# Two places for the weights of single expert blocks, an earlier second layer near the end, and a bias gated on ScalarE in a fused attention and mixture-of-experts kernel

## The chip, the cores and the metric

The kernel runs on one core of one Trainium2 chip. The metric is the device time of one execution in microseconds (us). All arithmetic is in fp32. The engines are named as the profile names them: PE (TensorE matmuls), PEld (TensorE weight loads), DVE (VectorE), ACT (ScalarE), POOL (GpSimd) and SP (SyncE, which here issues most of the DMAs).

## The reference

The input x holds 32 batches of 112 tokens with D = 256. The first layer is a gated cross-attention: its latents are the layer norm of x, its keys and values come from 375 context rows and the 112 latents (487 in all), with 16 heads of 64. The second layer is a feed-forward layer with 8 experts, of which each token takes two. What matters for the change is this second layer:

```
xf = layernorm(x).reshape(3584, 256)
scores = softmax(xf @ gate_w); top 2 of 8, divided by their sum
h = gelu(einsum('td,edf->etf', xf, w1) + b1)      # exact gelu, F = 1024
y = einsum('etf,efd->etd', h, w2) + b2
out = sum over the token's two experts of score * y
x = x + tanh(g_ffn) * out
```

## The kernel before

After the attention stage each token's row is scattered to a DRAM array `xg`, once for each of its two experts, so that the rows of an expert lie together. A row carries its 256 values, its gate (column `D`) and the number of its token (column `D + 1`). The expert stage then works through units of rows in an order fixed ahead. Which expert a unit belongs to is read from a table at run time (`number`, the register loads of `L1028`).

There are 21 **pairs** (`PAIRS = 21`, units 0 to 20) of 2 x 128 rows. They use a scheme of seven products of blocks where plain multiplication takes eight (`hidden_pair` and `second_pair`, whose matmuls are `L1255` and `L1317`), with sums of weights made earlier (`ws1`, `ws2`). After them come 18 **single blocks** of 128 rows (`SURE = 18`, units 21 to 38), computed plainly. `hidden(t)` makes the 1024 hidden values in 8 columns of 128, two matmuls each (`L1367`), and each column has a gelu with its bias on ACT (`L1374`). `second(t)` sums 8 matmuls into one bank (`L1382`). The trace has two rows for each of these fp32 matmuls: 32 for `hidden`, 16 for `second`. `combine(t)` adds the bias b2 on DVE (`L1232`), multiplies by the row's gate on DVE (`L1234`), and lets POOL issue a scatter-add of the 128 rows to the output (`add_rows`, `L1207`). The scatter-adds follow one another: each waits until the one before it has landed, since two blocks can hold the same token. Up to three more blocks stand behind a `tc.If`; they are not executed with these inputs.

**Weights.** A single block's weights are four halves of 512 KB: the first layer's two (hidden columns 0 to 511 and 512 to 1023) in the tiles `w_s23` and `w_12_22`, the second layer's two in `t14` (called `b1x`) and `b2x`. Each tile has one buffer, and `w_s23`, `w_12_22`, `t14` and `b2x` are the tiles of the pairs too. The trace shortens their names: `w_s` is `w_s23`, `w` is `w_12_22`, `w_t` is `t14`. SP issues the loads: `fetch_first` (`L1119`) for the first layer, `fetch_second` (`L1135`) for the second. From the second single block on each is conditional: it is done only where the block's expert differs from that of the block before. The loads of a half wait until the matmuls that read the same place are over. `found["w1"]` and `w2_first` are two further places of 1 MB each that held the weights of unit 0 and lie idle afterwards.

**Order.** The instructions of each engine run in the order in which the program writes them (`manual_schedule`). For a single block t the loop `run` writes `hidden(t)`, then the fetch of the first layer of t+1, the transposes of its rows (`turn_rows`, `L1158`, copied by DVE at `L1162`), `second(t - 1)` and `combine(t - 1)`, then the fetch of the second layer of t, and the rows of t+3. ACT issues the loads of the biases (`L1074` for b1, `L1077` for b2) and of the rows (`L1057`), in its queue between the gelus. After the last block `second` and `combine` of block 38 follow directly on those of 37:

```python
        def run(begin, end):
            for t in range(begin, end):
                hidden(t)
                if t + 1 < end:
                    fetch_first(t + 1)
...
                    second(t - 1)
                    combine(t - 1)
                fetch_second(t)
                rows_ahead(t, end)
            second(end - 1)
            combine(end - 1)
```

PSUM's eight banks are used in turn, one for each column of `hidden`. The tiles of the blocks (`hid`, `xsT`, `y`) have two buffers each.

## Time and profile before

| | us |
|---|---|
| median of 3 runs | 1871.33 |
| lowest and highest run | 1870.01, 1871.95 |
| the profiled execution | 1865.82 |
| its span in the profile | 1864.0 |

The mean granted clock of PE was 0.999 of full speed. In the profile a line of a group of instructions gives source line, engine, operation, output <- inputs with the names of the program, and the count; then busy time and the mean of one in ns. A line of the timeline gives its start, its duration, its engine, its line and operation, the number of instructions run together, and in brackets how long the engine had been idle before it and what ended that. `SPq` and `ACTq` are the queues of SP and ACT, where DMAs are issued. The duration of such a row is that of the issue and not of the transfer.

### The profile page before, as it was taken

Reading aid. Unit: us, or ns where it says so; the run is one execution under the profiler, and the core shown is the slowest. Engines: PE = TensorE matmul, PEld = TensorE weight load, DVE = VectorE, ACT = ScalarE, POOL = GpSimd, SP = SyncE. Lnnn points to the kernel's source line nnn. Section 1 sums busy time; section 2 is a strip of 40 time slices with the busy share of each in tenths; the row PEclk is TensorE's granted clock in tenths of the full one; section 3 lists DMA queues with packets and bytes.
Section 4 is the critical chain, followed back from the end, with each engine's and each line's share of the span. In section 5 each row is a group of like instructions: output and inputs, shape, how many; then the busy total and the mean of one; then the engine's idle time right before and its main releaser. Section 6 shows DMA issues by size and latency. Waiting matters only on the chain. (4 is left out here: it accounts for less than half of the span.)

```text
span 1864.0 us, 37204 instructions
## 1 busy us (share of the span) xinstructions
PE 1843.0 (99%) x12336; PEld 1410.6 (76%) x12336; DVE 1377.0 (74%) x2898; ACT 1131.8 (61%) x2718; POOL 969.0 (52%) x1361
## 2 busy tenths in 40 slices
PE   8999999999999999999999999999999999999998
PEld 4667777676677677767677767777677999999887
DVE  6888887888887878788878787888776477754111
ACT  4776666666676767676767676766656344434333
POOL 6433342525354846484556655662334688877212
PEclk9999999999999999999999999999999999999999
DMA  6577767666878888989898988897548876997872
GB/s 207 203 248 250 246 215 235 222 225 205 257 272 252 305 271 275 284 283 306 275 282 276 283 289 285 261 311 241 211 171 295 269 218 179 283 347 213 247 187 42
DMA packets 389747, 462.51 MB, mean 248 GB/s; under 512 B 142984, under 2 KB 279472, under 8 KB 373168
## 3 DMA queue, kind: packets, MB, share of 16 engines
q1 hardware_dynamic: 359568, 432.19, 70.0%
q0 software_dynamic: 11328, 15.33, 4.2%
q10 hardware_dynamic: 18656, 12.58, 2.5%
q8 instruction: 99, 1.62, 0.4%
q14 instruction: 96, 0.79, 0.1%
HBM read 316.05 MB, written 186.96 MB: 270 GB/s over the span
## 5 line engine op out<-in xcount | busy, mean ns | idle before, releaser
L592 ACT ACTIVATE ex<-bank,nmx 128x512 f32<-128x512 f32 x512 | 344.0, 698 | 86.2 <-DVE nmx L583 86.2
L606 ACT ACTIVATE ex<-ex,rc 128x512 f32<-128x512 f32 x512 | 345.1, 730 | 59.4 <-DVE rc L603 58.8
L583 DVE TENSOR_REDUCE nmx<-bank 128x1 f32<-128x487 f32 x512 | 298.3, 655 | 69.8 <-PE bank L573 69.3
L611 DVE STREAM_TRANSPOSE ex<-ex 128x1024 f32<-128x1024 f32 x256 | 314.1, 1227 | 20.3 <-ACT ex L606 20.2
L524 POOL TENSOR_TENSOR vv<-tmpv,vv 128x512 f32<-128x512 f32 x64 | 82.0, 1281 | 403.9 <-ACT vv L512 393.1
L573 PE MATMUL bank<-kT,qTs 64*128 64x487 f32 x1024 | 234.2, 583 | 0.8 <-ACT outT L652 0.3
L635 PEld LDWEIGHTS bank<-exT,vv 128*64 128x64 f32 (+1 forms) x4096 | 197.5, 136 | 29.5 <-issue 24.8
L652 ACT COPY outT<-bank 128x256 f32<-128x256 f32 (+3 forms) x160 | 40.0, 314 | 289.1 <-PE bank L635 289.1
L635 PE MATMUL bank<-exT,vv 128*64 128x112 f32 (+1 forms) x4096 | 211.3, 260 | 0.0
L471 PE MATMUL bank<-tT,wkv_s 128*128 128x487 f32 x378 | 186.5, 576 | 0.5 <-ACT ex L592 0.5
L476 PE MATMUL bank<-wkv_s,tT 128*128 128x256 f32 x768 | 186.5, 379 | 0.0
L476 PEld LDWEIGHTS bank<-wkv_s,tT 128*128 128x128 f32 x768 | 145.8, 190 | 44.0 <-issue 22.5
L1452 POOL TENSOR_TENSOR piece<-piece 128x128 f32<-128x128 f32 x256 | 117.2, 458 | 109.6 <-DMA piece<-in_L_ffn_w_dram 98.3
L573 PEld LDWEIGHTS bank<-kT,qTs 64*128 64x128 f32 x1024 | 98.4, 186 | 95.8 <-issue 70.7
L1207 POOL DMA_INDIRECT out_dram<-y,xs x60 | 93.6, 1559 | 148.7 <-DVE y L1234 64.8
L476 PEld LDWEIGHTS bank<-wkv,kvT 128*128 128x128 f32 x512 | 95.8, 190 | 56.3 <-issue 33.4
L476 PE MATMUL bank<-wkv,kvT 128*128 128x256 f32 x512 | 131.7, 380 | 0.8 <-ACT ex L592 0.6
L471 PE MATMUL bank<-kvT,wkv 128*128 128x487 f32 x252 | 130.1, 598 | 0.0
L521 DVE TENSOR_TENSOR vv<-bank,vv 128x512 f32<-128x512 f32 x192 | 123.4, 668 | 6.9 <-POOL vv L524 6.9
L521 DVE TENSOR_TENSOR kT<-bank,kT 128x487 f32<-128x487 f32 x189 | 116.8, 640 | 15.5 <-PE bank L471 15.2
L1262 ACT ACTIVATE h<-h,b 128x256 f32<-128x256 f32 x160 | 66.1, 495 | 89.5 <-DVE h L1275 89.5
L410 PEld LDWEIGHTS bank<-kvT,wq_sb 128*128 128x128 f32 x512 | 96.8, 190 | 28.1 <-issue 17.0
(299 smaller groups left out, 3654.9 us busy)
## 6 DMA issues: line engine op xcount, KB each, us to landing
turned<-ex SPq DMA_DIRECT2D x128, 1024.0 KB
exT<-turned SPq DMA_DIRECT2D x128, 1024.0 KB
w_t<-ws SPq DMA_DIRECT2D x40, 512.0 KB
w<-in_L_ffn_w_dram SPq DMA_DIRECT2D x38, 512.0 KB
w_b2x<-in_L_ffn_w_dram SPq DMA_DIRECT2D x38, 512.0 KB
ws<-piece SPq DMA_DIRECT2D x64, 256.0 KB
turned_in<-inputs SPq DMA_DIRECT2D x28, 512.0 KB
kvT<-turned_in SPq DMA_DIRECT2D x224, 64.0 KB
```

What stands on the lines that cost most here:

```text
L410: nc.tensor.matmul(ps, lhsT=wq_sb[:, k, i * P : (i + 1) * P], rhs=kvT[g][:, k, :, :S], start=(k == 0), stop=(k == KD - 1),)
L471: nc.tensor.matmul(ps, lhsT=w[:, 0, i * P : (i + 1) * P], rhs=x[:, :NK], start=True, stop=True)
L476: nc.tensor.matmul(ps[:, c, :], lhsT=x[:, (2 * h + c) * P : (2 * h + c + 1) * P], rhs=w[:, 1, i * P : (i + 2) * P], start=True, stop=True,)
L521: nc.vector.tensor_tensor(v[o], ps, v[r], ALU.add)
L573: nc.tensor.matmul(ps[:, :NK], lhsT=qT[b // 2, i][r, b % 2].rearrange("p a i -> p (a i)"), rhs=kT[b, i][r, :], start=True, stop=True,)
L583: nc.vector.tensor_reduce(nmx[b, i][:, j : j + 1], pss[b, i][j][:, :NK], AX.X, ALU.max, negate=True)
L592: nc.scalar.activation(exs[n % EXB][:, :, p, :, j, :], ps[j].rearrange("p (c r k) -> p k c r", c=NCK, r=QW), AF.Exp, bias=nmx[b, i][:, j : ...
L606: nc.scalar.mul(t, t, rc[:, j : j + 1])
L611: nc.vector.transpose(t, t)
L635: nc.tensor.matmul(ps[y * DH : (y + 1) * DH, r, x * S : (x + 1) * S].rearrange("p (a i) -> p a i", a=QB), lhsT=vv[j // 2, c // 2][:m, c % ...
L1207: add = nc.gpsimd.indirect_dma_start(out=outf, out_offset=bass.IndirectOffsetOnAxis(ap=xs[t][:, b, D + 1 : D + 2].bitcast(I32), axis=0), i ...
L1452: nc.gpsimd.tensor_tensor(o, l, r, op) for o, l, r, op in ops
```

## The change

The change has four parts, in the single blocks.

- The first half of each layer's weights gets two places, used by turns. With i = t - 21, the first layer's is a half of `found["w1"]` for even i and `w_s23` for odd i; the second layer's is a half of `w2_first` for even i and `t14` for odd i. The second halves stay in `w_12_22` and `b2x` (for i = 0 in the other halves of `found["w1"]` and `w2_first`). The second half is loaded if the expert differs from the block before. The first half is loaded if the expert of this block or of the block before is new, since its place was filled two blocks ago. Blocks 21 and 22 are loaded in any case.
- The order of the loads moves. All four halves of block 21 are issued at pair 18. The two first-layer halves of block 22 are issued at pair 20. In `run`, after `hidden(t)` come the second half of the first layer of t+1 and the first half of the first layer of t+2; after `second(t - 1)` come the second half of the second layer of t and the first half of the second layer of t+1. New functions `single`, `fetch_single` and `biases_of_single` do this; `single` loads three registers on SP where there were two.
- In the last turn of `run`, `second(37)` and `combine(37)` stand ahead of `hidden(38)`.
- Ahead of `second(t)`, ACT writes b2 times the gate into the unused half of the tile `y` (`gated_bias`); DVE then makes y from the bank, the gate and that half in one instruction instead of two.

```diff
@@ -1064,7 +1064,7 @@
             m, i = unit_of(t)
             e = number(m, i, 0, E - 1, (ET.SP, ET.Activation) if t > 1 else (ET.SP,))
 
-            new = {} if t in (0, 1, EARLY, PAIRS) else {"cond": number(m, i, 2, 1)}
+            new = {} if t in (0, 1, EARLY) else {"cond": number(m, i, 2, 1)}
             return e, new
 
         def fetch_biases(t, e, pool, n, layers=(0, 1)):
@@ -1101,20 +1101,14 @@
 
             e, new = found["e", t] = found.pop(("next", t), None) or expert_of(t)
             fetch_biases(t, e, found["weights"], 2, (0,))
-            if t < PAIRS:
-                s1_, s4_ = (
-                    (n, ws1[bass.ds(e, 1), place].rearrange("o p f -> p (o f)"))
-                    for n, place in (("s1", 3), ("s4", 2))
-                )
-                s23 = "s23", ws1[bass.ds(e, 1), 0:2].rearrange("o s p f -> p (o s) f")
-                order_ = (
-                    ("11", half_of_w1(e, 0, 0)), s23, s1_, ("12_22", rows_of_w1(e, 1)), s4_
-                )
-            else:
-                if t == PAIRS:
-                    wt["11"], wt["12"] = (wt["s23"][:, n] for n in range(2))
-                    wt["21"], wt["22"] = (wt["12_22"][:, n] for n in range(2))
-                order_ = ("s23", columns_of_w1(e, 0)), ("12_22", columns_of_w1(e, 1))
+            s1_, s4_ = (
+                (n, ws1[bass.ds(e, 1), place].rearrange("o p f -> p (o f)"))
+                for n, place in (("s1", 3), ("s4", 2))
+            )
+            s23 = "s23", ws1[bass.ds(e, 1), 0:2].rearrange("o s p f -> p (o s) f")
+            order_ = (
+                ("11", half_of_w1(e, 0, 0)), s23, s1_, ("12_22", rows_of_w1(e, 1)), s4_
+            )
             for n, src in order_:
                 nc.sync.dma_start(wt[n], src, **new)
 
@@ -1122,15 +1116,8 @@
 
             e, new = found.pop(("e", t))
             b2x = "b2x", half_of_w2(e, 1, 0, D)
-            if t < PAIRS:
-                planes = ws2[bass.ds(e, 1)].rearrange("o (a b) p c d -> b p (o a) (c d)", b=2)
-                order_ = ("b11", half_of_w2(e, 0, 0, P)), b2x, ("t14", planes[0]), ("t32", planes[1])
-            else:
-                if t == PAIRS:
-                    wt["b1x"] = wt["t14"].rearrange("p a f -> p (a f)").rearrange(
-                        "p (c d) -> p c d", d=D
-                    )
-                order_ = ("b1x", half_of_w2(e, 0, 0, D)), b2x
+            planes = ws2[bass.ds(e, 1)].rearrange("o (a b) p c d -> b p (o a) (c d)", b=2)
+            order_ = ("b11", half_of_w2(e, 0, 0, P)), b2x, ("t14", planes[0]), ("t32", planes[1])
             for n, src in order_:
                 nc.sync.dma_start(wt[n], src, **new)
             fetch_biases(t, e, found["weights"], 2, (1,))
@@ -1141,6 +1128,30 @@
 
             e, _ = expert_of(0)
             nc.sync.dma_start(w2_first, w2[bass.ds(e, 1)].rearrange("o (c p) d -> p (o c) d", p=P))
+
+        def single(t, cond=True):
+
+            i = t - PAIRS
+            e = number("c", i, 0, E - 1, (ET.SP, ET.Activation))
+            one = two = {}
+            if cond and i > 1:
+                one = number("c", i, 2, 1)
+                one, two = {"cond": one}, {"cond": one | number("c", i - 1, 2, 1)}
+            H = NF // 2
+            room = found["w1"].rearrange("p k (h f) -> p h k f", h=2)
+            b1x = wt["t14"].rearrange("p a f -> p (a f)").rearrange("p (c d) -> p c d", d=D)
+            wt["w1", t] = [(room[:, 0], wt["s23"])[i % 2], wt["12_22"] if i else room[:, 1]]
+            wt["w2", t] = [(w2_first[:, :H], b1x)[i % 2], wt["b2x"] if i else w2_first[:, H:]]
+            found["one", t] = e, two, one
+
+        def fetch_single(t, layer, h):
+            e, *new = found["one", t]
+            dst = wt[("w1", "w2")[layer], t][h]
+            src = columns_of_w1(e, h) if layer == 0 else half_of_w2(e, h, 0, D)
+            nc.sync.dma_start(dst, src, **new[h])
+
+        def biases_of_single(t, layer):
+            fetch_biases(t, found["one", t][0], found["weights"], 2, (layer,))
 
         def weights_ahead():
 
@@ -1227,11 +1238,20 @@
             n = 2 if t == 0 else 1
             sums = found.pop("sums", [])
             do(sums[:1])
-            y = found["tiles"].tile([P, 2, D], F32, tag="y", name=f"y_{t}")
+            y = ys.pop(t, None)
+            if y is None:
+                y = found["tiles"].tile([P, 2, D], F32, tag="y", name=f"y_{t}")
             for b in range(n):
-                nc.vector.tensor_tensor(y[:, b], psy.pop((t, b)), bias[t][1], ALU.add)
-                give((t, b))
-                nc.vector.tensor_scalar(y[:, b], y[:, b], xs[t][:, b, D : D + 1], None, ALU.mult)
+                gate = xs[t][:, b, D : D + 1]
+                if t < PAIRS:
+                    nc.vector.tensor_tensor(y[:, b], psy.pop((t, b)), bias[t][1], ALU.add)
+                    give((t, b))
+                    nc.vector.tensor_scalar(y[:, b], y[:, b], gate, None, ALU.mult)
+                else:
+                    nc.vector.scalar_tensor_tensor(
+                        y[:, b], psy.pop((t, b)), gate, y[:, 1], ALU.mult, ALU.add
+                    )
+                    give((t, b))
                 added = add_rows(t, b, y[:, b])
                 if n == 2:
                     do(sums[b + 1 : b + 2])
@@ -1363,10 +1383,10 @@
             for f in range(NF):
                 ps = psum(P)
                 h, c = divmod(f, NF // 2)
-                for k, w in enumerate((("11", "12"), ("21", "22"))[h]):
+                for k in range(KD):
                     nc.tensor.matmul(
                         ps,
-                        lhsT=wt[w][:, c * P : (c + 1) * P],
+                        lhsT=wt["w1", t][h][:, k, c * P : (c + 1) * P],
                         rhs=xsT[t][:, k, 0, :],
                         start=(k == 0),
                         stop=(k == KD - 1),
@@ -1375,14 +1395,19 @@
                     hid[t][:, f, :], ps, AF.Gelu, bias=bias[t][0][:, f : f + 1]
                 )
 
+        def gated_bias(t):
+            y = ys[t] = found["tiles"].tile([P, 2, D], F32, tag="y", name=f"y_{t}")
+            nc.scalar.mul(y[:, 1], bias[t][1], xs[t][:, 0, D : D + 1])
+
         def second(t):
+            gated_bias(t)
             ps = psy[t, 0] = psum(D, hold=(t, 0))
             for f in range(NF):
                 h, c = divmod(f, NF // 2)
                 nc.tensor.matmul(
                     ps,
                     lhsT=hid[t][:, f, :],
-                    rhs=wt[("b1x", "b2x")[h]][:, c, :],
+                    rhs=wt["w2", t][h][:, c, :],
                     start=(f == 0),
                     stop=(f == NF - 1),
                 )
@@ -1854,9 +1879,15 @@
         for t in range(1, PAIRS):
             if t > 1:
                 hidden_pair(t)
-                fetch_first(t + 1)
                 if t + 1 < PAIRS:
-                    found["next", t + 2] = expert_of(t + 2)
+                    fetch_first(t + 1)
+                    if t + 2 < PAIRS:
+                        found["next", t + 2] = expert_of(t + 2)
+                else:
+                    biases_of_single(PAIRS, 0)
+                    single(PAIRS + 1)
+                    fetch_single(PAIRS + 1, 0, 0)
+                    fetch_single(PAIRS + 1, 0, 1)
                 turn_rows(t + 1, nc.scalar.copy)
                 if t + 1 < PAIRS:
                     rows_sums(t + 1)
@@ -1871,6 +1902,11 @@
             if t + AHEAD == EARLY:
                 do(outgoing)
                 del outgoing[:]
+            if t == PAIRS - 3:
+                single(PAIRS)
+                for layer in range(2):
+                    for h in range(2):
+                        fetch_single(PAIRS, layer, h)
             rows_ahead(t)
             for _ in range(2 if t == 2 or t + AHEAD > EARLY - 3 else int(t > 1)):
                 do(outgoing[:1])
@@ -1879,19 +1915,34 @@
 
         def run(begin, end):
             for t in range(begin, end):
+                ahead_ = begin < t == end - 1
+                if ahead_:
+                    second(t - 1)
+                    combine(t - 1)
                 hidden(t)
                 if t + 1 < end:
-                    fetch_first(t + 1)
+                    if t > PAIRS:
+                        fetch_single(t + 1, 0, 1)
+                    biases_of_single(t + 1, 0)
+                if t + 2 < end:
+                    single(t + 2)
+                    fetch_single(t + 2, 0, 0)
+                if t + 1 < end:
                     turn_rows(t + 1)
-                    if t + 2 < end:
-                        found["next", t + 2] = expert_of(t + 2)
                 if t == PAIRS:
                     second_pair(t - 1)
                     out_pair(t - 1)
-                else:
+                    biases_of_single(t, 1)
+                elif not ahead_:
                     second(t - 1)
                     combine(t - 1)
-                fetch_second(t)
+                if t > PAIRS + 1:
+                    fetch_single(t, 1, 1)
+                if t + 1 < end:
+                    fetch_single(t + 1, 1, 0)
+                    biases_of_single(t + 1, 1)
+                if t == PAIRS:
+                    fetch_single(t + 1, 1, 1)
                 rows_ahead(t, end)
             second(end - 1)
             combine(end - 1)
@@ -1902,8 +1953,11 @@
         with tc.If(more):
             for t in range(PAIRS + SURE, PAIRS + NS):
                 fetch_rows(t)
-                fetch_first(t)
-                fetch_second(t)
+                single(t, False)
+                for layer in range(2):
+                    biases_of_single(t, layer)
+                    for h in range(2):
+                        fetch_single(t, layer, h)
                 turn_rows(t)
                 hidden(t)
                 second(t)
```

## Prediction, made before the changed kernel ran

> **What bounds the kernel now.** I read the page first, then the distances between the starts of single blocks in the timeline, the waits of TensorE, the table by stretches, and last the chain of waits. The page:
>
> ```profile
> PE 1843.0 (99%) x12336; PEld 1410.6 (76%) x12336; DVE 1377.0 (74%) x2898; ACT 1131.8 (61%) x2718; POOL 969.0 (52%) x1361
> ```
>
> PE limits, and its clock is full, so only two things can change the time: gaps of PE, and what follows its last matmul. The change touches the blocks 21 to 38, so I took the start of each block's first `L1367` row. An unstalled period is 7.25 us. From block 23 (1729.47) to block 34 (1816.61) there are eleven periods: 87.14 us where 11 x 7.25 = 79.75 would do. So 7.39 us are lost, and from block 34 on nothing. The waits of PE in that stretch:
>
> ```profile
> PE bank L1382 <- DMA w_t<-in_L_ffn_w_dram: 2.1, 2, 1.3
> PE bank L1367 <- DMA w_s<-in_L_ffn_w_dram: 1.4, 2, 1.2
> PE bank L1367 <- DVE y L1234: 1.0, 1, 1.0
> PE bank L1367 <- DMA w<-in_L_ffn_w_dram: 0.7, 1, 0.7
> PE bank L1382 <- DMA w_b2x<-in_L_ffn_w_dram: 0.2, 1, 0.2
> ```
>
> (total, times, longest.) Nearly all are weights. The wait on `DVE y` is one too: it ends at 1785.90 while that y was done 1.0 us before; a w_s load issued at 1779.47 is what is left. The timeline gives the age of a late load:
>
> ```profile
> 1759.51 0.37 SPq L1135 DMA_DIRECT2D w_t<-in_L_ffn_w_dram  x1
> ...
> 1766.29 1.97 PE L1382 MATMUL bank<-w_t,h 128*128 128x256 f32 x8 [1.29 <-DMA w_t<-in_L_ffn_w_dram]
> ...
> 1795.20 0.37 SPq L1119 DMA_DIRECT2D w_s<-in_L_ffn_w_dram  x1
> ...
> 1801.79 2.02 PE L1367 MATMUL bank<-xsT,w_s 128*128 128x128 f32 x16 [1.16 <-DMA w_s<-in_L_ffn_w_dram]
> ```
>
> From issue to use 6.78 and 6.59 us, where the place is free only some 5.4 us ahead of the use. An issue of 0.37 us is a load, one of 0.07 or 0.08 a skipped one; by these rows new experts begin at blocks 23, 24, 26, 27, 28, 30 and 32. Splitting the lost time by the half whose use starts late, against an unstalled block: first halves 1.13, 0.43, 1.52, 1.16, 1.32, 0.25 = 5.81 us; second halves 0.95, 0.42 = 1.37; rest 0.21. The table by stretches (us; PE, PEld, DVE, ACT, POOL busy; clock, DMA share, GB/s):
>
> ```profile
> 1656.00:1672.00 16.00, 16.00 (x146) 16.00 (x145) 7.33 (x16) 7.04 (x18) 12.75 (x16) 1.00 1.07 355
> ...
> 1688.00:1704.00 16.00, 16.00 (x146) 16.00 (x145) 9.89 (x20) 5.32 (x13) 12.76 (x12) 1.00 0.75 225
> ...
> 1761.05:1769.82 8.77, 7.48 (x52) 6.86 (x51) 1.20 (x3) 2.94 (x8) 1.54 (x1) 1.00 1.06 314
> ...
> 1785.90:1793.22 7.32, 7.32 (x51) 6.91 (x51) 0.42 (x1) 2.54 (x8) 1.54 (x1) 1.00 0.30 58
> ```
>
> The engines of the DMAs alternate between full (314) and empty (58). The end, by the chain of waits:
>
> ```profile
> 1853.97 1.54 DMA out_dram<-y,xs
> 1855.51 2.83 issue
> 1858.35 0.50 POOLq L1028
> 1858.85 1.25 POOL out_dram L1207
> ```
>
> and the timeline at the same place:
>
> ```profile
> 1856.27 0.42 DVE L1232 TENSOR_TENSOR y<-bank,b 128x256 f32<-128x256 f32 x1 [2.58 <-PE bank L1382]
> 1856.73 0.35 DVE L1234 TENSOR_SCALAR y<-y,xs 128x256 f32<-128x256 f32 x1
> 1858.55 1.54 POOL L1207 DMA_INDIRECT out_dram<-y,xs  x1 [3.04 <-DVEq L1902]
> ```
>
> The last y is ready at 1857.08, but its scatter-add starts at 1858.55: it waits for block 37's, started only at 1853.97. Elsewhere it follows y by about 0.3 us.
>
> **The change part by part.** All is reckoned on the profiled execution, 1865.82 us (span 1864.0, 1.82 around it), which is 5.51 below the median of the runs, 1871.33; I put the difference on the median.
>
> *First halves in two places.* The place of block t's first halves was used by t-2, so the window grows from about 5.4 to about 11 us (one period less the loads' own distance). The oldest late load above took 6.8 us, so the 5.81 us go to nothing. The cover is over 4 us.
>
> *Second halves.* Their place is still one, and their window still about 5.4 us. Block 21's four halves and 22's come early; there are 14 loads in the blocks 23 to 32. What is late next is these. Before, they cost 1.37 / 14 = 0.10 us each, but the first halves' stalls gave them time; the first halves, with the same window and nothing ahead to shelter them, cost 5.81 / 14 = 0.42. The second halves now stand ahead of the pair's first half in SP's queue, but behind the previous pair. I take 0.3, nearer to the unsheltered row: 14 x 0.3 = 4.2, bounds 1.4 and 5.8. Of 7.18 us, 2.98 are saved (bounds 1.4 and 5.8).
>
> *More bytes.* With two places every new expert loads its first half twice. Counting done issues, 7 halves of 0.524 MB are added, 3.67 MB, to the 20.7 MB that moved from 1722.22 to 1816.61 (the rates above times their stretches; 220 GB/s over 94.39 us). Blocks 23, 26 and 27 then ask for four halves in a period, 2.10 MB in 7.25 us = 289 GB/s, below the 314 of the best single-block stretch and 355 of the pairs. So I put no separate price on it; the rival below has it.
>
> The Trainium skill, "DMA: Bandwidth & Descriptors", Specifications, gives a limit of about 358 GB/s for one core's HBM traffic. The 355 row stands at it, and by that limit alone four halves in a period would fit and all second halves be in time, a saving of 7.2 us. Its section "Latency and other measured facts" speaks against the change: HBM access latency goes from 0.2 us to 2 us at high load, and the change fills the empty stretches; by it, each second half might come up to 1.8 us later. The late loads of 6.6 to 6.8 us agree in direction; no row here isolates it.
>
> *Early loads at pair 18.* Four issues of 0.37 us and 2.10 MB go on SP's queue at about 1688, where SP now issues block 21's rows (1688.39, used over 15 us later), and behind the second-layer loads of pair 18 (the last issued by 1687.65). Pair 20's expert is that of 19 (its issues are skipped), so the burst falls into the 225 GB/s stretch; at 355 it takes 5.9 us, to about 1694.3. The next loads are pair 19's second layer, issued from 1693.61 to 1700.5 and used from 1705.09 to 1710: I cost it at nothing. Were that cover gone and they came a whole burst later, the w_b2x half (issued 1698.81, used 1705.98, 7.2 us; late loads need 6.7) would cost 5.9 - 0.5 = 5.4 us. Block 21 had no weight wait, so nothing is gained there.
>
> *SP's register work.* Three register loads for a block instead of two, and some nine rows more for a block (0.03 to 0.5 us each by the `MOVE` and `L1028` rows, at most about 1 us). They stand ahead of a first half, which has over 4 us to spare, and behind the second half.
>
> *Bias on ScalarE.* 18 more ACT rows, between 0.31 us (`L652`, 128x256 copy) and 0.50 (`L1262`, 128x256), where ACT idles 3.75 us a block. It now waits for y's buffer, i.e. for the scatter-add of block t-2 to land (3.7 to 7.4 us from its issue), and for b2. Behind it in ACT's queue are the row and bias loads and the next block's gelus; PE waits for those gelus to free a bank. In blocks 22 to 25 the adds run late (y of 21 is done at 1730.53, its add starts at 1737.42), so ACT may be held up to some 1.5 us; PE bears about 2.6 us, as its banks take most of a hidden layer (an estimate from the eight banks and the 0.45 us a hidden column takes). I take zero, with up to 3 us lost if the adds fall a further block behind. VectorE has two rows (0.42 and 0.35) replaced by one like `L1343` (0.48).
>
> *Second layer of block 37 ahead of 38's first.* PE does the same matmuls. Its add starts about 3.5 us earlier and has landed when the last y is ready. The last add then follows y by 0.3 instead of 1.47 us: 1.17; and y comes 0.81 - 0.48 = 0.33 earlier. Together 1.5 us, bounds 0.4 (PE meets 0.8 to 1.1 us of gelu latency between the two layers of 38, which the moved layer used to cover) and 1.9.
>
> Sum: 2.98 + 1.5 = 4.5 us; 1871.33 - 4.5 = 1866.8 (profiled 1861.3). Its own range: 1871.33 - 5.8 - 1.9 = 1863.6 to 1867.6, which is the bound of a visible gain: 0.2%, 3.74 us, is about what a measurement of this kernel can tell from no change.
>
> **The rivals.** *Gain given back, no visible change.* Second halves cost what the first halves did, 0.42 each: 1.4 + 1.5 = 2.9 saved, 1868.4; with a further gelu wait of 1 to 3 us, up to 1872. For it: the waits move in kind from one half to the other, and the window is equal. Against: half of the loads are no longer urgent, so fewer are in flight together.
>
> *DMA rate becomes the bound, slower.* The place is blocks 23 to 28, five new experts in six blocks with up to four halves each. 24.4 MB have to move in that stretch. At R GB/s it takes 24.4 / R: with the tail's 1.5 us, over 0.2% slower begins at 94.39 + 5.24 = 99.6 us, i.e. R below 245 GB/s; 235 gives 103.8 us, +9.4 - 1.5 = +7.9, 1879. For it: the mean is 220 now, and full single-block stretches show 268, 287 and 314 with waits in them. Against: the mean holds empty stretches of 58, which early loads fill, and pairs hold 350 for 48 us. At 255 it would be 95.7 us, 1871.2.
>
> *The doubled loading is not doing what it says:* if conditions let nothing be skipped, 2.10 MB in all 16 periods, still 289 GB/s; it belongs to the rival above.
>
> **How the numbers follow.** Forecast, visible gain: 0.50. No visible change: 0.25, mostly 1868 to 1872. Slower: 0.25, of which the DMA rate 0.15, around 1877 to 1879, and the rest a late pair 19 or held gelus on top of unchanged waits, 1875 to 1877. The range that leaves out 2 in 10 runs from 1863.4 to 1877.0; the forecast's own is 1863.6 to 1867.6.
>
> **What would show it.** Right: no `L1387` wait on w_s, and the odd first halves of the second layer never waited for; what is left stands on `w`/`w_12_22` and b2x; eleven periods from block 23 sum to about 84 us; the last scatter-add starts 0.3 us after its y. Wrong: waits on `L1387` and `L1407` of 10 us or more with stretches of two blocks held at 235 to 250 GB/s; a PE gap between 1690 and 1711; or ACT idle behind the y buffer with PE waiting on gelu.

## The result, and the profile after

The changed kernel is slower: 1877.51 us median of 20 runs (1871.16 to 1885.53) against 1870.62 for the kernel before (20 runs, 1867.16 to 1872.87). The ratio is 1.0041, 95% interval 1.0033 to 1.0050, or 7.7 us. The profiled execution took 1874.37 us, its span is 1872.6; it is 3.1 us faster than the median, so the profile shows less of the loss than the times do. The page, and the waits of PE from pair 19 on (total, times, longest; `L1337` is the second layer of pairs, `L1387` and `L1407` the two layers of single blocks, which were `L1317`, `L1367` and `L1382`):

```profile
PE 1846.3 (99%) x12336; PEld 1412.0 (75%) x12336; DVE 1371.6 (73%) x2880; ACT 1139.1 (61%) x2736; POOL 969.4 (52%) x1361
```

```profile
PE bank L1407 <- DMA w_b2x<-in_L_ffn_w_dram: 4.3, 4, 1.8
PE bank L1387 <- DMA w<-in_L_ffn_w_dram: 2.7, 3, 1.7
PE bank L1337 <- DMA w_b2x<-in_L_ffn_w_dram: 2.1, 1, 2.1
PE bank L1337 <- DMA w_b<-in_L_ffn_w_dram: 0.8, 1, 0.8
```

As predicted, no wait on `w_s`, `w_t` or the spare places is left: every first half is in time. What is late is the second halves (`w`, `w_b2x` of `L1387` and `L1407`), and, new, pair 19's second layer. (The trace also writes `w` for the first half in `found["w1"]`; by the timeline all three waits of `L1387` stand in the middle of a block's first layer, ahead of the second half.) The starts of the stages in the two profiles (us):

| | before | after | difference |
|---|---|---|---|
| start of `hidden_pair(20)` | 1698.62 | 1701.80 | +3.18 |
| from there to `hidden(21)` | 12.73 | 18.04 | +5.31 |
| `hidden(21)` to `hidden(23)` | 18.12 | 18.12 | 0 |
| `hidden(23)` to `hidden(34)` | 87.14 | 88.76 | +1.62 |
| `hidden(34)` to the end | 47.42 | 45.84 | -1.58 |

The first row is not the change's. It arises where the attention ends: from the ScalarE instruction at 1401.7 of before to that at 1524.0, the same work took 122.2 to 123.6 us in twelve of the 20 profiles (before's among them) and 125.9 to 127.4 in eight (after's among them), and each chip below showed one of the two for all its kernels. The ratios compare runs on one chip, so it falls out of them. It may also be most of the 5.51 us by which before's profiled execution lay under the median in the prediction.

**Pair 19.** The waits of SP in the 22 us around the early halves, first after, then the same stretch of before:

```profile
SPq L1113 <- DMA w<-in_L_ffn_w_dram: 3.0, 2, 1.5
SPq L1122 <- DMA w_b2x<-in_L_ffn_w_dram: 1.5, 1, 1.5
SPq L1113 <- DMA ex<-in_L_ffn_w_dram: 1.3, 1, 1.3
```

```profile
SPq L1135 <- PE bank L1317: 5.8, 2, 4.5
SPq L1119 <- PE bank L1255: 3.9, 4, 1.8
```

Before, SP waits for PE to free a place. After, it waits for loads to land. `L1113` is pair 20's first layer, whose five loads are skipped and need nothing; `ex` is the spare place `w2_first`. The timeline after:

```profile
1694.47 3.54 SPq L1057 DMA_DIRECT2D xs<-xg  x1
...
1699.83 0.08 SPq L1113 DMA_DIRECT2D w<-in_L_ffn_w_dram  x1
...
1705.95 0.38 SPq L1122 DMA_DIRECT2D w_b<-in_L_ffn_w_dram  x1
...
1709.21 1.13 PE L1337 MATMUL bank<-w_b,h 128*128 128x128 f32 x8 [0.78 <-DMA w_b<-in_L_ffn_w_dram]
...
1712.44 1.16 PE L1337 MATMUL bank<-w_b2x,h 128*128 128x128 f32 x8 [2.09 <-DMA w_b2x<-in_L_ffn_w_dram]
1713.73 2.08 PE L1337 MATMUL bank<-w_t,h 128*128 128x128 f32 x8
```

Before, `w_b` was issued at 1693.61; moved by the 3.18 us that this profile is behind, that is 1696.8. It now goes out at 1705.95, 9.2 us late. The trace's records of the issues say why. The loads of SP and ScalarE signal their landing on eight semaphores (counters; the expectations below call them the ring), taken in turn, and an issue first waits until the earlier load on its semaphore has landed. A skipped load takes its turn too. Four skipped loads of pair 20 had the four semaphores of the early halves. Three of these halves landed at 1699.71, 1701.58 and 1703.30, and SP went on at 1699.73, 1701.60 and 1703.31; it went on from the fourth at 1705.41, the last record of whose landing is missing. So the 2.10 MB took 14.0 us from their first issue at 1691.38.

The two waits of PE are 2.9 us of the 5.31. Behind the second one TensorE was granted half its clock for 3.41 us (the number before the last two is the clock):

```profile
1713.58:1716.99 3.41, 3.28 (x16) 3.27 (x16) 0.00 (x0) 0.00 (x0) 0.00 (x0) 0.50 1.07 358
```

Two groups of eight matmuls there take 2.08 and 1.72 us where 1.06 is usual, and the starts behind them lie 1.63 us later than at the usual 0.89 us a group. The remaining 0.8 us are lost where TensorE starts again after the two waits.

**The end** went as forecast. The last y and its scatter-add:

```profile
1866.44 0.48 DVE L1251 SCALAR_TENSOR_TENSOR y<-bank,xs,y 128x256 f32<-128x256 f32 x1 [6.54 <-PEq L1953]
1867.20 1.54 POOL L1218 DMA_INDIRECT out_dram<-y,xs  x1 [4.24 <-DVE y L1251]
```

y is done at 1866.92 and the add starts 0.28 us later, where it was 1.47.

### The profile page after: what moved, and what is told of

The parts are those of the page before. It is cut to its first block, busy times and chain, and to the rows that moved or that the text cites. A ratio compares the mean times of both kernels' runs of the same rounds, so it can differ in the third digit from the quotient of the medians.

```text
span 1872.6 us, 37381 instructions
## 1 busy us (share of the span) xinstructions
PE 1846.3 (99%) x12336; PEld 1412.0 (75%) x12336; DVE 1371.6 (73%) x2880; ACT 1139.1 (61%) x2736; POOL 969.4 (52%) x1361
## 3 DMA queue, kind: packets, MB, share of 16 engines
q8 instruction: 99, 1.62, 0.3%
```

## The experiments

All were timed in five rounds against the kernel before on their chip; "us" below is (ratio - 1) x before's median there. "Gaps" is what blocks 23 to 33 lose against 11 x 7.25 us in that kernel's one profile. It varies from execution to execution: burst_late's profile is of its fastest execution, and late_y3 has more gaps than burst_late in the profiles but less time. "Chip" numbers the five groups that were timed together, each on one chip. late_one_copy and late_one_copy_y3 leave out loads that the right result needs, so they are no versions to use.

| kernel | chip | ratio, 95% interval | us | `hidden_pair(20)` to `hidden(21)` | gaps | from `hidden(34)` |
|---|---|---|---|---|---|---|
| before | - | 1 | 0 | 12.73 | 7.39 | 47.42 |
| after | - | 1.0041, 1.0033-1.0050 | +7.7 | 18.04 | 9.01 | 45.84 |
| tail_only | 1 | 0.9989, 0.9981-0.9998 | -2.1 | 12.72 | 7.28 | 46.07 |
| no_skips | 1 | 1.0026, 1.0012-1.0040 | +4.9 | 12.80 | 17.94 | 45.72 |
| burst_late | 1 | 1.0019, 1.0006-1.0031 | +3.6 | 12.73 | 8.12 | 45.81 |
| bias_back | 1 | 1.0053, 1.0037-1.0068 | +9.9 | 16.87 | 14.49 | 45.92 |
| late_one_copy | 2 | 0.9980, 0.9970-0.9990 | -3.7 | 12.72 | 5.65 | 46.06 |
| late_rows_pool | 2 | 0.9995, 0.9985-1.0005 | -0.9 | 12.72 | 10.13 | 46.10 |
| tail_gate | 2 | 1.0003, 0.9991-1.0015 | +0.6 | 12.73 | 8.60 | 46.43 |
| late_bias_back | 2 | 1.0034, 1.0017-1.0050 | +6.4 | 12.72 | 13.67 | 46.24 |
| late_pool27 | 3 | 1.0021, 1.0010-1.0033 | +3.9 | 12.73 | 13.40 | 45.92 |
| late_rows_early | 3 | 1.0008, 0.9999-1.0017 | +1.5 | 13.13 | 10.28 | 45.80 |
| late_y3 | 3 | 0.9988, 0.9979-0.9997 | -2.2 | 12.73 | 9.08 | 45.86 |
| late_early_y3 | 3 | 1.0011, 0.9999-1.0023 | +2.1 | 12.73 | 9.94 | 45.79 |
| late_one_copy_y3 | 4 | 0.9974, 0.9964-0.9984 | -4.9 | 12.72 | 3.18 | 45.70 |
| tail_y3 | 4 | 1.0006, 0.9997-1.0015 | +1.1 | 12.72 | 8.06 | 46.40 |
| tail_gate_y3 | 4 | 1.0005, 0.9996-1.0015 | +0.9 | 12.72 | 8.10 | 46.62 |
| late_again | 5 | 1.0037, 1.0017-1.0056 | +6.9 | 12.72 | 9.56 | 45.83 |
| late_y3_again | 5 | 0.9995, 0.9987-1.0004 | -0.9 | 12.73 | 5.99 | 45.84 |
| tail_again | 5 | 0.9998, 0.9990-1.0007 | -0.4 | 12.72 | 8.27 | 46.21 |

### The end alone: tail_only

```diff
# the kernel before
+                ahead_ = begin < t == end - 1
+                if ahead_:
+                    second(t - 1)
+                    combine(t - 1)
                 hidden(t)
...
-                else:
+                elif not ahead_:
                     second(t - 1)
                     combine(t - 1)
```

> The kernel before with one edit: second and combine of block 37 stand ahead of hidden of block 38. In the profiles of before and after the stretch from the start of hidden(34) to the end of the span is 147.39 and 145.88 us, 1.51 less. Theory: the reorder alone gives the 1.2 us of the scatter-add that no longer waits, the bias on ScalarE the other 0.3. Expected: 1.2 us faster than before (1869.4), that stretch at about 146.2 us, the last scatter-add 0.3 us after its y. Rival: the reorder exposes the gelus between the two layers of block 38, 0.8 us or more of PE gap, and the gain came from the shorter VectorE path: 0.4 us or less.

The end fell by 1.35 us in the profile, to 46.07, and the time by 2.1 us (0.4 to 3.6). The reorder brings nearly all of the gain at the end; the rival of an exposed gelu is out. Timed once more (tail_again) the end is 1.21 us shorter than before's, but the time only 0.4, within the noise.

### Pair 19: no_skips, burst_late

```diff
# no_skips: the changed kernel, fetch_first
-            for n, src in order_:
+            for n, src in order_ if t != PAIRS - 1 else ():
# burst_late: the changed kernel
-            if t == PAIRS - 3:
+            if t == PAIRS - 2:
                 single(PAIRS)
-                for layer in range(2):
-                    for h in range(2):
-                        fetch_single(PAIRS, layer, h)
+            if t > PAIRS - 3:
+                for h in range(2):
+                    fetch_single(PAIRS, t + 2 - PAIRS, h)
```

> The changed kernel without the five conditional first-layer loads of pair 20, which are skipped with these inputs and move no byte. Theory L (order on SP): SP does not issue a load until the load that used the same completion semaphore, eight loads back, has landed, and a skipped load takes its turn too; so the five skipped ones made SP wait for the four early halves of block 21, and pair 19's second-layer loads were issued 9 us late (w_b at 1705.95, where before, shifted by the 3.2 us that this profile lies behind, it would be 1696.8). Without the skipped loads they go out about 5 us sooner, and the PE gap in pair 19's second layer falls from 5.3 us to under 1.5: 4 to 5 us faster than the changed kernel, about 1873. Theory R (rate): the 2 MB of early halves fill the transfer engines, and the loads behind them are late whatever the order; the same bytes move, the gap stays at 4 us or more, and the time at about 1877.

> The changed kernel with block 21's first-layer halves loaded one pair later (pair 19, behind its second-layer loads) and its second-layer halves two pairs later (pair 20), instead of all four at pair 18. Both theories of the gap in pair 19 (waits for landings on SP, or the rate of the transfers) say it goes: 5.3 us less than the changed kernel, about 1872.2, if block 21's own loads, issued some 10 us ahead of their use, are in time. If they are late, up to 3 us of it comes back. What then is left against before is the single blocks (+1.6 in the profiles) and the end (-1.5): no difference from before within 0.1%. Rival: the whole slowdown lies in the single blocks, and nothing changes (1877).

Without the skipped loads the gap of pair 19 is gone: 12.80 us instead of 18.04, with the same bytes at the same place. The timeline of no_skips, whose `hidden_pair(20)` starts 1.41 us later than after's:

```profile
1701.86 0.37 SPq L1122 DMA_DIRECT2D w_b<-in_L_ffn_w_dram  x1
...
1703.81 0.37 SPq L1122 DMA_DIRECT2D w_b2x<-in_L_ffn_w_dram  x1
...
1709.69 1.06 PE L1337 MATMUL bank<-w_b,h 128*128 128x128 f32 x8
```

`w_b` is issued 5.5 us sooner against the stage, and PE does not wait. So it was SP's order that made pair 19 late, not the rate of the transfers; that was even higher here over the 14 us from the first early issue (324 GB/s, 297 after). The row load's issue takes 3.31 us here too, without harm. The whole time fell by only 2.8 us, under the 4 to 5 expected and with intervals that overlap, and the profile shows 17.94 us of gaps in the single blocks: these vary much from run to run (below). burst_late removes the gap as well and gains 4.1 us (3.6 instead of 7.7), but it stays slower than before, which "no difference within 0.1%" had not allowed; timed once more (late_again) it gains only 0.8. So the 5.3 us are shown by the profiles and not by the whole times, in which the single blocks cost more than the first profile's +1.6.

### The bias: bias_back, late_bias_back, tail_gate

bias_back is the changed kernel with the two VectorE instructions of before; late_bias_back is the same on burst_late; tail_gate is tail_only with `gated_bias` and the one VectorE instruction of the changed kernel.

> The changed kernel with the bias of the single blocks added and gated on VectorE in two instructions, as before. Theory L: on ScalarE the gated bias waits for the scatter-add of two blocks ago, the load of the rows stands behind it in ScalarE's queue, and SP's load of a first half waits for those rows to land (eight loads back); w_s at 1753.98 was issued 4 us after its place was free, and urgent halves stood behind it. Without it the gaps of PE in blocks 23 to 33 fall from 9.0 us to 6 to 8, the end loses 0.3, so 1 to 3 us faster than the changed kernel: 1874.5 to 1876.5. Theory R: the gaps come from bytes alone; they stay at 9 us, and with 0.3 us more at the end it is 1877.8.

> The variant with block 21's halves loaded late, and the bias of the single blocks on VectorE as before. The changed kernel with that bias alone measured 1881.7, not better than with it on ScalarE. If the bias on ScalarE costs nothing in the single blocks: 1873.5, the late variant's 1873.2 and 0.3 us at the end. If it holds the row loads and through them SP: 1870.5 to 1872. If VectorE's two rows were the worse (the copy of the next block's rows stands behind them): above 1875.

> The kernel before with the two small parts of the change and none of its loads: second and combine of block 37 ahead of hidden of 38, and the bias gated on ScalarE. The reorder alone measured 2.0 us below before (1869.1). If the bias costs nothing it adds 0.3 us at the end: 1868.8, within 0.5 us of the reorder alone. If ScalarE's wait for the scatter-add of two blocks ago holds the gelus and the row loads behind it, the gaps of blocks 23 to 33 grow by 1 to 3 us and it lies at 1870 to 1872.

The first two missed: with the bias back on VectorE it is not faster, and by the ratios slower (9.9 against 7.7, 6.4 against 3.6, intervals overlapping; late_again's 6.9 takes the second difference away). SP still waits for rows there, 10.3 us in bias_back's trace. The reason is in the queue of ScalarE: the changed order loads b2 of t+1 one block earlier, into the buffer that `combine(t - 1)` reads; with the bias on VectorE that `combine` waits for the scatter-add (12.1 us in three waits), and the b2 load, with the row load behind it, waits for `combine`: one issue of b2, ready at 1779.31, goes out at 1783.61. So taking the gated bias away did not take the wait away. Whether VectorE's two rows cost something besides is not shown. tail_gate, 1.0003, lies 2.7 us above tail_only's first measurement and 1.0 above its second (tail_again), so a cost of the bias without the new loads is not shown.

### The bytes: late_one_copy

```diff
# burst_late, in single
-                one, two = {"cond": one}, {"cond": one | number("c", i - 1, 2, 1)}
+                one = {"cond": one}
+                two = one
```

> The variant with block 21's halves loaded late, and the first halves loaded only where the block itself has a new expert: the second copy, for the other place one block later, is not loaded, so every other block of an expert computes with a first half of an older expert. What is left out is 7 half loads of the blocks 23 to 33 (3.7 MB); every load that stays is issued at the same place in the order. Theory B (bytes): the doubled first halves are what makes the second halves late. The gaps of blocks 23 to 33 fall to 5 us or less, 2.5 us or more under the kernel before's 7.4; with 1.5 us of the end the time is 1.5 to 4 us below before (1867 to 1869.5), against 2.1 us above with the bytes. Theory W (waits on SP): loads go out late because SP waits for the landing of loads eight turns back, skipped ones among them; taking bytes away changes little, the gaps stay at 7 us or more and the time at before's or above (1871 to 1873).

Without the second copies burst_late falls from +3.6 to -3.7 us, intervals far apart, though from two chips. The table by stretches for blocks 23 to 33, of before, after and late_one_copy (last column GB/s):

```profile
1729.47:1816.61 87.14, 81.72 (x551) 74.89 (x550) 13.22 (x33) 30.54 (x88) 18.53 (x12) 1.00 0.78 215
```

```profile
1737.96:1826.72 88.76, 81.73 (x551) 75.17 (x550) 9.99 (x22) 34.12 (x99) 18.54 (x12) 1.00 0.87 257
```

```profile
1729.12:1814.52 85.40, 80.96 (x552) 75.04 (x551) 9.99 (x22) 35.97 (x99) 18.53 (x12) 1.00 0.83 217
```

18.7, 22.8 and 18.5 MB. With two places and the bytes of before, 5.65 us of gaps are left where before loses 7.39, a little over the 5 expected. So the second copies turn the idea over. Leaving them out takes away bytes and, with them, landings that later issues wait for; this run does not separate the two.

### How the bytes cost time: rows and buffers

Three kernels move the row loads of burst_late. late_rows_pool issues those of blocks 24 to 38 on GpSimd, late_pool27 from 27 on; late_rows_early puts them ahead of `second(t - 1)` and so of the gated bias in ScalarE's queue. late_y3 gives y three buffers; late_early_y3 has three buffers and the rows ahead.

```diff
# late_rows_pool, in fetch_rows
+            if PAIRS + AHEAD <= t < PAIRS + SURE:
+                at, eng = ET.Pool, nc.gpsimd
# late_y3, wherever y is allocated
-tag="y", name=f"y_{t}")
+tag="y", name=f"y_{t}", bufs=3)
```

> The variant with block 21's halves loaded late, and the row loads of the blocks 24 to 38 issued by GpSimd instead of ScalarE. They then leave the ring of eight completion semaphores that the loads of SP and ScalarE share, and SP's first-half load no longer waits for rows to land (up to 4 us each in the traces); six loads a block remain in the ring. No byte changes. Theory W: SP is no longer held, the gaps of blocks 23 to 33 fall by 2 us or more, 1869 to 1871. Theory B: unchanged, 1872.5 to 1874. Rival: the rows come late behind the scatter-adds on GpSimd, and it is slower than 1875.

> As the variant with the rows on GpSimd, but only from block 27 on: in its profile the rows of block 24 came late behind the lagging scatter-adds and cost one 5.9 us gap, while the periods from block 24 to 34 lost only 4.2 us (late variant 8.0, before 6.4). Theory W (SP held by the landing of rows in the ring): without that gap the blocks 23 to 33 lose 5 us or less, and the time is 2 to 5 us below before (ratio 0.9973 to 0.999). Rival: the gap of block 24 was bad luck of one execution and the gain of 4.5 us in the times came from somewhere before block 27: ratio 1.000 or above.

> The variant with block 21's halves late, and the row loads of t+3 on ScalarE ahead of the gated bias of t-1 and of the load of b2 instead of behind them. Same loads, same ring, same bytes. Chain theory: ScalarE waits for the scatter-add of t-3 before the gated bias, the row load stood behind that, and SP's first-half load waits eight turns back for those rows; moved ahead, the rows go out when the gelus are done, SP waits for them no more, and it gains 3 us or more against the late variant (ratio 1.0019): 0.9985 to 1.000. Ring theory without the add: it is the number of loads in the ring and their landing times, so the order on ScalarE changes nothing: 1.0015 to 1.003.

> The variant with block 21's halves late, and three buffers for y instead of two: the gated bias of block t waits for the scatter-add of t-3, not of t-2. Chain theory (scatter-add, then ScalarE, then rows, then SP): the adds lag by up to a block and a half, one more buffer takes the wait away, and it gains 3 us or more against the late variant: ratio 0.9985 to 1.000. Ring theory without the add: 1.0015 to 1.003.

> Both: row loads ahead of the gated bias, and three buffers for y. Chain theory: each alone takes the wait away, so together no more than the better of the two, ratio 0.998 to 0.9995. If the two work on different waits (rows to SP, gelus to PE) they add up: 0.997.

The chain that these test stands in the waits of ScalarE and SP between 1725 and 1835 (us in total, times, longest). After, and then no_skips, the execution with the widest gaps:

```profile
ACT y L1400 <- DMA out_dram<-y,xs: 18.5, 5, 4.5
```

```profile
ACT y L1400 <- DMA out_dram<-y,xs: 40.0, 9, 6.7
```

The gated bias waits for the landing of a scatter-add. The row load stands behind it in ScalarE's queue, and in no_skips SP waits for those rows to land:

```profile
SPq L1151 <- DMA xs<-xg: 22.3, 6, 4.3
```

and its timeline shows one turn:

```profile
1789.83 0.51 ACT L1400 ACTIVATE y<-b,xs 128x256 f32<-128x256 f32 x1 [5.85 <-DMA out_dram<-y,xs]
...
1791.24 0.42 ACTq L1057 DMA_DIRECT2D xs<-xg  x1
...
1797.85 3.49 PE L1407 MATMUL bank<-w_b2x,h 128*128 128x256 f32 x8 [3.41 <-DMA w_b2x<-in_L_ffn_w_dram]
...
1800.62 0.51 ACT L1400 ACTIVATE y<-b,xs 128x256 f32<-128x256 f32 x1 [6.69 <-DMA out_dram<-y,xs]
```

The scatter-adds of this stretch took 9.1 and 10.1 us from issue to landing, longer than a block, and each starts only when the one before has landed. The 3.49 us of the `L1407` row, 1.89 elsewhere, are TensorE at half its clock again. In blocks 23 to 33 such a stretch of 3.41 us or more follows a long wait of PE (1.9 to 4.5 us) in the profiles of no_skips, burst_late, late_again, bias_back, tail_gate_y3, both kernels with rows on GpSimd and both with the rows ahead; there is none in before, after, late_y3 and late_one_copy, nor behind a wait of 3.0 us in late_bias_back. At half the clock 3.41 us cost about 1.7 (an estimate: half of them), which is part of the spread of the gaps.

late_rows_pool (-0.9) fits the chain, late_pool27 (+3.9) does not. Why is open: the rows of the first crowded blocks, 24 to 26, stay on ScalarE in late_pool27, but PE waits once for late rows in both profiles (4.0 and 3.8 us for `xs`). late_rows_early (+1.5) gains 2.1 us, less than expected: SP hardly waits for rows any more (0.5 us) but 6.8 us for b2. late_y3 gained 5.8 us against burst_late on another chip; late_early_y3 (+2.1), expected at late_y3's time or below, did not, with b2 waited for by SP again (3.6 us).

### One chain or two costs

late_one_copy_y3, tail_y3 and tail_gate_y3 are the kernels of those names with three buffers for y; the three "again" kernels are burst_late, late_y3 and tail_only on one chip.

> The variant with block 21's halves late, without the second copy of the first halves (every other block of an expert computes with an older first half; 7 half loads are left out), and with three buffers for y. Against the late variant (1.0019), leaving out the copies measured 7.3 us less and three buffers 5.8 us less. If these are one chain (the extra bytes make the scatter-adds land late, ScalarE waits for them, and loads and gelus go out late behind it), three buffers add little without the extra bytes: 0.997 to 0.9985, within 1.5 us of leaving out the copies alone (0.998). If they are separate costs they add up: 0.995 or below.

> The kernel before with block 37's second layer ahead of 38's first and three buffers for y; bias on VectorE, loads as before. The reorder alone measured 0.9989. In before VectorE waits for the scatter-add of t-2 where ScalarE waits in the changed kernel; nothing urgent stands behind VectorE's wait but the copy of the next block's rows. If the wait costs only on ScalarE: 0.9985 to 0.9993, no more than the reorder. If it costs here too: 0.9975 or below, and this is the best version.

> The kernel before with the reorder at the end, the bias on ScalarE, and three buffers for y; loads as before. Reorder and bias with two buffers measured 1.0003, the reorder alone 0.9989. If the wait of ScalarE for the scatter-add is what the bias costs, three buffers take it away: 0.998 to 0.9988, 0.3 us or more below the reorder alone. If the cost is something else on ScalarE (one more instruction behind the gelus): 0.9995 to 1.0005.

> The variant with block 21's halves late, once more, now on one chip with its own version with three buffers for y and with the reorder alone; the earlier ratios of these (1.0019, 0.9988, 0.9989) come from two chips, and three buffers did not help in the other variants. If the ratios carry over from chip to chip: 1.0006 to 1.0031 again.

> The same with three buffers for y. If ScalarE's wait for the scatter-add is a cost of its own: 3 us or more below the late variant on this chip, as before. If not: within 1.5 us of it, and the single 0.9988 was the chip or the other stages.

> The kernel before with block 37's second layer ahead of 38's first, once more: 0.9981 to 0.9998 if it carries over; by the profiles (1.35 us at the end) 0.9993. If it is at or below the other two, it is the best version that computes everything.

On one chip late_y3 is 7.8 us below the late variant, with intervals apart (+6.9 and -0.9), and its profiles hold no wait of ScalarE for a scatter-add: with the doubled loads and two buffers of y, most of the time goes behind that wait. Without the doubled loads three buffers bring 1.2 us (late_one_copy_y3) or nothing (tail_gate_y3 against tail_gate; tail_y3, slower than either case expected). So the doubled loads and the second buffer cost together what neither costs alone. A smaller price of the loads is left: with three buffers they lie 2.7 and 4.0 us above late_one_copy_y3. The rate is not the limit: late_y3_again moves the doubled loads faster than any of the others, and is not slower than before:

```profile
1729.06:1814.80 85.74, 81.38 (x551) 74.88 (x550) 9.99 (x22) 35.42 (x99) 18.53 (x12) 1.00 0.91 265
```

How the loads and the buffer meet is in part argued: the extra loads make the scatter-adds land late, and with two buffers of y that holds ScalarE, and behind it the rows, b2 and gelus, and through the row loads SP. The adds do land later, 5.3 us from issue in the median in before and 4.9 in late_one_copy, 5.6 in late_again and 6.2 in late_y3_again. But ScalarE's wait for them is shorter in the one profile of burst_late than in that of late_one_copy:

```profile
ACT y L1400 <- DMA out_dram<-y,xs: 12.3, 4, 5.2
```

```profile
ACT y L1401 <- DMA out_dram<-y,xs: 14.4, 5, 4.0
```

It is longer in after (18.5 us) and no_skips (40.0). Why late_early_y3 lies above late_y3 is open too. tail_only and late_y3 lie at or below before both times, by 0.4 to 2.2 us; neither is faster in both by its interval, so no version that computes everything is shown to beat before by 0.2%.

## Why the prediction was wrong

- **First halves to nothing, new waits on the second halves:** right, no first half is late in the profile after.
- **The end:** right in the profiles. 1.5 us forecast, 1.58 in the profile, 1.35 of it from the reorder (tail_only; 1.21 in tail_again).
- **Early loads at pair 18, "I cost it at nothing":** the step that failed first, 5.3 us in the profile. Cover was sought in the rate: the burst was to land in 5.9 us and took 14.0, and the loads behind it were taken to be issued when before issued them. SP was held by the landing of the burst itself, through skipped loads that I counted at 0.08 us. no_skips shows it. The price without cover, 5.4, was met by luck: it stood for one late half, and what was lost is 2.9 us of waits, 1.6 at half the clock and 0.8 in starting again. That a wait of PE also costs clock had no term in the prediction.
- **Second halves at 0.3 us each, saving 2.98 us:** failed. In the profiles of the kernels with doubled loads and two buffers of y (after, no_skips, burst_late, late_again, bias_back, late_bias_back, both with rows on GpSimd, late_rows_early) blocks 23 to 33 lose 8.1 to 17.9 us, 11.8 in the mean. In six profiles with the loads of before it is 7.3 to 8.6, mean 8.0. So instead of 3.0 saved, 3.9 are lost. In late_one_copy, without the second copies, 1.7 us are saved (5.65 against 7.39), above the lower bound of 1.4 but not the 2.98.
- **More bytes at no price of their own:** failed; the doubled loads are most of the step above. The rate was not what decided: 257 GB/s in the profile after and 265 in late_y3_again lie above the rival's bound of 245. In no_skips it was 232, but there ScalarE and SP waited 40.0 and 22.3 us as shown above. The loads cost by lateness, of urgent halves and of scatter-adds.
- **Gated bias at zero, up to 3 us "if the adds fall a further block behind":** right in its mechanism, and the adds did fall behind; its size was wrong. late_again and late_y3_again differ by 7.8 us, burst_late and late_y3 by 5.8. The prediction priced only the gelus behind the wait; rows, b2 and, through the rows, SP's loads stand behind it too. How much each of these costs is not shown.

The sum with these: 5.3 + 3.9 - 1.6 = 7.6, against 7.7 measured. That it meets so closely is in part luck: 3.9 is a mean over unlike kernels, and after's own profile gives 5.3 + 1.6 - 1.6 = 5.3. The time fell in the rival "slower", which I had put on the rate and, in a smaller part, on a late pair 19; the end of the range, 1877.0, lies 0.5 us below the time.

The rule weighed in the prediction, of the Trainium skill's "DMA: Bandwidth & Descriptors", section "Latency and other measured facts", that latency grows with load, agrees in direction: a scatter-add took 3.7 to 7.4 us from issue to landing in before and up to 10.1 in no_skips. The limit of about 358 GB/s in the page's section "Specifications", by which the second halves would have been in time, did not tell the outcome: 257 were moved, and they were late.

## What to carry to other kernels

A prefetch is not free because its bytes fit: follow each queue past it, and ask what the next issue waits for. Loads that share a few completion semaphores in turn, skipped ones among them, can make an early, unhurried load hold back a later, urgent one; put it behind the urgent ones, or leave the skipped ones out. Where a compute engine gets a wait for a transfer, count all that stands in its queue, and give the buffer that it waits for one more copy before adding bytes.

## What was not expected of the hardware

- An issue on SP itself can stretch: the row load's took 3.54 us after (3.31 in no_skips) with the early halves under way, and 0.34 us in before.
- One load can hang on a few of its 16 parts: in bias_back a w_b2x half issued at 1782.88 had 13 of them landed after 3.98 us and the last after 9.91, and PE waited 4.51 us for it. Such late parts may explain some of the spread of the single blocks' gaps; how much is open.
- A wait of TensorE can cost more than its length: after waits of 1.9 to 4.5 us its granted clock was half for 3.41 us at least in ten of the 20 profiles, but not after every such wait.
